# Output product of a state-space scan: seven block products per pair of tiles instead of eight

## The chip, the cores and the metric

The kernel runs on one core of a Trainium2 chip. The metric is the device time of one execution in microseconds. A core has a matrix engine (PE, with its weight loads listed as PEld), a vector engine (DVE), a scalar engine (ACT), a general engine (POOL) and a queue engine that here issues the loads (SP). Each engine runs its own instructions in the order in which they were placed on it, and waits on semaphores for the others.

## The reference, cut to what matters

The program is one layer: a graph part, a state-space scan, and a feed-forward part, each added to the residual `x`. The change lies in the scan alone. Of the scan this matters (16 sequences of 32 tokens, 512 model columns, 8192 inner columns in 8 groups of 1024):

```
proj = jnp.einsum('bsd,od->bso', h, in_proj_w)
gate = proj[..., :D_INNER]
hBC = jax.nn.silu(causal_conv(proj[..., D_INNER:D_INNER + CONV_DIM], conv_w, conv_b))
...
M = jnp.einsum('bcihn,bcjhn->bcijh', Ch, Bh) * jnp.transpose(L, (0, 2, 3, 4, 1))
Y_diag = jnp.einsum('bcijh,bcjhp->bcihp', M, hc)
...
y = (Y_diag + Y_off).reshape(b, S, H_M, P_M)[:, :s] + D_res
yg = y.reshape(b, s, D_INNER) * jax.nn.silu(gate)
ygr = yg.reshape(b, s, G_M, gsz)
ygr = ygr * jax.lax.rsqrt(jnp.mean(ygr * ygr, axis=-1, keepdims=True) + EPS)
y = ygr.reshape(b, s, D_INNER) * gnorm_w
out = jnp.einsum('bsd,od->bso', y, out_proj_w)
return residual + out
```

A sequence fits in one chunk, so no state passes between chunks. The last product, `out`, is 512 tokens by 8192 inner columns by 512 model columns in f32, and it is the one that the change computes in another way.

## The kernel before

**Tiling.** Inner columns lie on the 128 partitions and the 512 tokens along the free axis. The 8192 inner columns are 64 tiles of 128, and a group (`g`, of 8) is `TG` = 8 tiles. The 512 tokens are four quarters `q` of 128. `xt` holds the residual, tokens on partitions, one 512-column slice per quarter.

**A group's three steps.** `inner(g)` projects and convolves: for each of 8 tiles, `project` (L1114) loads a 256 KB weight tile `win` on SP (six buffers) and makes four f32 products into one of two PSUM buffers of tag `p`, once for the gate and once for the hidden part. The gate's product goes through a Silu on ACT (L1199) into `gs`; the hidden product through ACT (L1127), three shifted multiply-adds on DVE (L1132) and a Silu (L1135) into `hid`. `gs` and `hid` have two buffers each, so two groups are alive at a time.

`mix(g)` makes the scan's values: per tile `i`, four transposes of `hid` on PE (`pht`, L1228, PSUM tag `m`), a scaling on DVE (`hd`, L1230), every second tile a decay table (`decays`: `da` on POOL L1208, `pl` on PE L1213 in tag `m`, `ed` by an exponential on ACT L1218), two products `el` on DVE (L1241), sixteen half-width records on PE (`py`, L1249, PSUM tag `y`), then on DVE the skip term (L1253) and the gating (L1254), on ACT the square (L1256, L1259) and the scaling by the norm weight (L1261), and on POOL the sum of squares `ssq` (L1260).

`close(g)` makes the group's part of the output: the sum over partitions of `ssq` on PE (`pn`, L1268, tag `y`), the factor `rs` from it on DVE and ACT, eight loads of `out_proj` tiles on SP (`wo`, L1276, ten buffers), and for each quarter eight accumulating f32 products of 128 x 128 by 128 x 512 into a PSUM buffer of tag `o` (`po`, L1281), which DVE scales by `rs` and adds to `xt` (L1284).

**Order.** The text's order is `inner(0)`, and then for each `g`: `inner(g + 1)`, `mix(g)`, `close(g)`. The order on each engine is not written out by hand. A planner puts the instructions on their engines ahead of the run, and the text's order is its priority. The PSUM has eight banks and the four tags `p`, `m`, `y`, `o` take two each, so all are spoken for.

Of the kernel before, what the change touches and what calls it, by code (L numbers as in the profile page):

```python
# [8 lines left out]
F32 = mybir.dt.float32  # L9
# [4 lines left out]
ALU = mybir.AluOpType  # L14
# [4 lines left out]
P = 128  # L19
B = 16  # L20
C = 32
D = 512
# [18 lines left out]
H_M, G_M, SEQ = 128, 8, 32  # L41
D_INNER = 8192
NT = D_INNER // P
TG = NT // G_M
# [8 lines left out]
def kernel(ctx: ExitStack, tc: tile.TileContext, I, out):  # L53
# [68 lines left out]
    with ExitStack() as cx:  # L122
        scan_part(nc, tc, cx, I, id32, ones, xt, U, rstd, lows)
# [931 lines left out]
def scan_part(nc, tc, cx, I, id32, ones, xt, u, rstd, lows):  # L1055
# [3 lines left out]
    wk = cx.enter_context(tc.tile_pool(name="swk", bufs=2))  # L1059
    sm = cx.enter_context(tc.tile_pool(name="ssm", bufs=3))  # L1060
    wpool = cx.enter_context(tc.tile_pool(name="sw", bufs=4))
    ps_p = cx.enter_context(tc.tile_pool(name="sps_p", bufs=2, space=PSUM))
    ps_m = cx.enter_context(tc.tile_pool(name="sps_m", bufs=2, space=PSUM))
    ps_y = cx.enter_context(tc.tile_pool(name="sps_y", bufs=2, space=PSUM))
    ps_o = cx.enter_context(tc.tile_pool(name="sps_o", bufs=2, space=PSUM))
# [82 lines left out]
    with tc.tile_pool(name="soft", bufs=1) as sp:  # L1148
# [11 lines left out]
        s2 = sp.tile([P, 4, H_M], F32, name="s2")  # L1160
        nc.vector.tensor_tensor(s2, s, s, ALU.mult)
        acc = sp.tile([P, 4, H_M], F32, name="acc")
# [29 lines left out]
    def inner(g):  # L1192

        gs = big.tile([P, TG, D], F32, tag="gs", name=f"gs{g}")
        hid = big.tile([P, TG, D], F32, tag="hid", name=f"hid{g}")
        for i in range(TG):
            t = g * TG + i
            pg = project(t, f"g{t}")
            nc.scalar.activation(gs[:, i], pg, AF.Silu)  # L1199
            convolve(hid[:, i], t, f"h{t}")  # L1200
            if g > 0:
                next(parts, None)
        return gs, hid

    def decays(h):

        da = sm.tile([P, 4, 4, SEQ], F32, tag="da", name=f"da{h}", bufs=2)
        nc.gpsimd.tensor_tensor(  # L1208
            da, lei.unsqueeze(1).unsqueeze(1).to_broadcast([P, 4, 4, SEQ]),
            dA[:, :, h:h + 4].rearrange("p q h -> p h q").unsqueeze(3).to_broadcast([P, 4, 4, SEQ]), ALU.mult,  # L1210
        )
        pl = ps_m.tile([P, 4, 4, SEQ], F32, tag="m", name=f"pl{h}")
        nc.tensor.matmul(  # L1213
            pl.rearrange("p h q i -> p (h q i)"), lhsT=gt, rhs=da.rearrange("p h q i -> p (h q i)"),
            start=True, stop=True,
        )
        ed = sm.tile([P, 4, 4, SEQ], F32, tag="ed", name=f"ed{h}", bufs=2)
        nc.scalar.activation(ed, pl, AF.Exp)  # L1218
        return ed

    def mix(g, gs, hid):

        ssq = wk.tile([P, D], F32, tag="ssq", name=f"ssq{g}")
        for i in range(TG):
            t = g * TG + i
            pt = ps_m.tile([P, 4, P], F32, tag="m", name=f"pht{t}")
            for q in range(4):
                nc.tensor.transpose(pt[:, q], hid[:, i, q * P:(q + 1) * P], id32)  # L1228
            hd = sm.tile([P, 4, 2, 64], F32, tag="hd", name=f"hd{t}")
            nc.vector.tensor_tensor(  # L1230
                hd, pt.rearrange("p q (h c) -> p q h c", h=2),
                dt[:, :, 2 * t:2 * t + 2].unsqueeze(3).to_broadcast([P, 4, 2, 64]), ALU.mult,
            )
            py = ps_y.tile([P, 4, P], F32, tag="y", name=f"py{t}")
            if i % 2 == 0:
                decay = decays(2 * t)
            els = []
            for j in range(2):

                el = sm.tile([P, 4, P], F32, tag="el", name=f"el{2 * t + j}")  # L1240
                nc.vector.tensor_tensor(  # L1241
                    el.rearrange("p q (b i) -> p q b i", b=4),
                    decay[:, 2 * (i % 2) + j].unsqueeze(2).to_broadcast([P, 4, 4, SEQ]),
                    CB[:, g].rearrange("p q (b i) -> p q b i", b=4), ALU.mult,
                )
                els.append(el)
            for q in range(4):
                for j in range(2):
                    nc.tensor.matmul(  # L1249
                        py[64 * j:64 * j + 64, q], lhsT=hd[:, q, j], rhs=els[j][:, q], start=True, stop=True  # L1250
                    )
            pyf = py.rearrange("p q t -> p (q t)")
            nc.vector.scalar_tensor_tensor(hid[:, i], hid[:, i], dpc[:, t:t + 1], pyf, ALU.mult, ALU.add)  # L1253
            nc.vector.tensor_tensor(gs[:, i], gs[:, i], hid[:, i], ALU.mult)  # L1254
            if i == 0:
                nc.scalar.activation(ssq, gs[:, i], AF.Square)  # L1256
            else:
                sq = wk.tile([P, D], F32, tag="sq", name=f"sq{t}")
                nc.scalar.activation(sq, gs[:, i], AF.Square)  # L1259
                nc.gpsimd.tensor_tensor(ssq, ssq, sq, ALU.add)  # L1260
            nc.scalar.activation(gs[:, i], gs[:, i], AF.Copy, scale=gnw[:, t:t + 1])  # L1261
        return ssq

    def close(g, gs, ssq):

        pn = ps_y.tile([P, 4], F32, tag="y", name=f"pn{g}")
        for q in range(4):
            nc.tensor.matmul(pn[:, q:q + 1], lhsT=ssq[:, q * P:(q + 1) * P], rhs=ones[:, 0:1], start=True, stop=True)  # L1268
        mean = sm.tile([P, 4], F32, tag="gm", name=f"gm{g}")
        nc.vector.tensor_scalar(mean, pn, 1.0 / (TG * P), None, ALU.mult)  # L1270
        rs = sm.tile([P, 4], F32, tag="gr", name=f"gr{g}")
        rstd(sm, rs, mean, 4, f"gn{g}")
        wo = []
        for i in range(TG):
            w = wpool.tile([P, D], F32, tag="wo", name=f"wo{g}_{i}", bufs=TG + 2)
            nc.sync.dma_start(out=w, in_=I["out_proj"][g * TG + i])  # L1276
            wo.append(w)
        for q in range(4):
            po = ps_o.tile([P, D], F32, tag="o", name=f"po{g}_{q}")
            for i in range(TG):  # L1280
                nc.tensor.matmul(  # L1281
                    po, lhsT=gs[:, i, q * P:(q + 1) * P], rhs=wo[i], start=(i == 0), stop=(i == TG - 1)
                )
            nc.vector.scalar_tensor_tensor(xt[:, q], po, rs[:, q:q + 1], xt[:, q], ALU.mult, ALU.add)  # L1284

    cur = inner(0)
    for g in range(G_M):
        nxt = inner(g + 1) if g + 1 < G_M else None
        ssq = mix(g, *cur)
        close(g, cur[0], ssq)  # L1290
        cur = nxt


# [140 lines left out]
```

## Time and profile before

| | us |
|---|---|
| three executions | 2415.48, 2420.97, 2423.53 |
| median of them | 2420.97 |
| the profiled execution | 2416.21 |
| its span, first to last instruction | 2414.5 |
| mean granted clock of PE over the span | 0.971 of full speed |

The scan runs from about 1370 us of the span to 2316 us. The groups follow one another at an equal distance: the eight `pn` stand at

| group | 0 | 1 | 2 | 3 | 4 | 5 | 6 | 7 |
|---|---|---|---|---|---|---|---|---|
| `pn` at, us | 1612.71 | 1716.34 | 1821.40 | 1926.58 | 2031.63 | 2136.68 | 2241.81 | 2296.60 |

From group 1 to group 6 that is 105.1 us a group. The last distance is short because no group's projections are left. In a row of the groups of instructions, the first number after the bar is busy time, then the mean of one in ns, then the idle time of the engine ahead of them with the engine that ended it. In a row of the timeline the first two numbers are the start and the length, and records of one line that follow each other are merged (x8). Starts of the products overlap the ends of the ones before, so the price of one is the distance between starts.

### The profile page before, as it was taken

How to read it: one execution, taken by the hardware profiler on the slowest of the kernel's cores; microseconds unless marked ns; L12 is line 12 of the kernel's file. 1: busy time of each engine (PE TensorE's matmuls, PEld its weight loads, DVE VectorE, ACT ScalarE, POOL GpSimd, SP SyncE). 2: the span in 40 equal slices, each digit the busy share in tenths (PEclk: the TensorE clock that was granted, in tenths of full speed). 3: DMA queues.
4: the chain of work that ended last, by engine and by line, in shares of the span. 5: the costliest groups of instructions: out<-in, count | busy, mean ns of one | idle time of the engine just before them, and what ended most of it. 6: DMA issues, size and time to landing. Idle time of an engine off the chain costs nothing. (4 is left out here: it accounts for less than half of the span.)

```text
span 2414.5 us, 88867 instructions
## 1 busy us (share of the span) xinstructions
PE 2190.0 (91%) x39234; PEld 1248.1 (52%) x39234; DVE 1699.6 (70%) x3674; ACT 1100.1 (46%) x2023; POOL 831.6 (34%) x897
## 2 busy tenths in 40 slices
PE   5699798999999778789999789999999999999979
PEld 2255455667676454567777544444444444444422
DVE  8487797888899888889999866554553625446643
ACT  6677566667665334345555322333332424333331
POOL 2165556445446565664655300020210202021200
PEclk9799899999999999999999899999999999999989
DMA  1323232132132231422211212213112121210000
GB/s 48 80 55 77 48 80 57 43 73 47 36 70 56 54 77 46 91 52 65 63 34 41 91 53 77 75 32 91 53 53 71 35 91 46 73 55 20 27 36 18
DMA packets 121625, 137.99 MB, mean 57 GB/s; under 512 B 18398, under 2 KB 79506, under 8 KB 121154
## 3 DMA queue, kind: packets, MB, share of 16 engines
q1 hardware_dynamic: 121240, 132.32, 21.9%
q8 instruction: 308, 5.05, 0.9%
q14 instruction: 77, 0.63, 0.1%
HBM read 77.02 MB, written 12.85 MB: 37 GB/s over the span
## 5 line engine op out<-in xcount | busy, mean ns | idle before, releaser
L849 POOL TENSOR_TENSOR EN<-e,rz 128x480 f32<-128x480 f32 x344 | 342.4, 995 | 554.4 <-DVE rz L847 430.1
L874 PE MATMUL u<-WA,DD 128*32 128x128 bf16 (+1 forms) x16512 | 418.6, 250 | 26.4 <-issue 26.4
L874 PEld LDWEIGHTS <-DD 128*32 128x32 f16 x16512 | 338.8, 98 | 72.7 <-issue 68.5
L879 ACT COPY us<-u 128x512 f32<-128x512 f32 x516 | 302.0, 587 | 149.5 <-PE u L874 131.8
L834 ACT ACTIVATE e<-s,smc 128x480 f32<-128x480 f32 x344 | 227.6, 662 | 290.7 <-PE s L829 248.0
L770 POOL TENSOR_TENSOR DD<-fs,crep 128x480 f16<-128x480 f32 (+2 forms) x344 | 349.6, 1017 | 0.0
L902 PEld LDWEIGHTS h<-e,us 128*32 128x32 f32 (+1 forms) x11008 | 248.8, 126 | 144.1 <-issue 65.6
L902 PE MATMUL h<-e,us 128*32 128x30 f32 (+1 forms) x11008 | 282.0, 211 | 37.1 <-DVE e L855 19.4
L821 DVE TENSOR_REDUCE c<-s 128x16 bf16<-128x480 f32 x344 | 220.7, 642 | 107.0 <-PE s L812 104.4
L1132 DVE SCALAR_TENSOR_TENSOR cyh<-ppch,t_conv_w,cyh 128x496 f32<-128x496 f32 (+2 forms) x192 | 137.4, 716 | 221.7 <-ACT cyh L1127 217.7
L1208 POOL TENSOR_TENSOR da<-lei,dA 128x512 f32<-128x512 f32 x32 | 40.6, 1269 | 611.8 <-PE pl L1213 577.5
L1281 PE MATMUL po<-wo,gs 128*128 128x512 f32 x512 | 240.5, 605 | 10.4 <-DVE xt L1284 10.3
L1120 PE MATMUL ppch<-hT,winch 128*128 128x512 f32 x512 | 232.2, 593 | 0.0
L1120 PE MATMUL ppg<-hT,wing 128*128 128x512 f32 x512 | 231.9, 593 | 0.0
L855 DVE STREAM_TRANSPOSE e<-EN 128x512 f32<-128x512 f32 x344 | 224.4, 652 | 0.0
L841 DVE TENSOR_REDUCE z<-e 128x16 f32<-128x480 f32 x344 | 219.5, 638 | 0.0
L539 ACT ACTIVATE sgn<-kd 128x512 bf16<-128x512 f32 x256 | 153.0, 598 | 56.2 <-PE kd L538 52.4
L812 PEld LDWEIGHTS <-DD 128*32 128x32 f16 x5504 | 81.7, 96 | 163.2 <-issue 129.5
L723 DVE TENSOR_SCALAR oh<-it,rank 128x512 bf16<-128x512 f16 x512 | 158.0, 368 | 7.5 <-PE pp L689 7.5
L812 PE MATMUL s<-DX,DD 128*32 128x120 f16 x5504 | 143.1, 223 | 19.6 <-DMA DX<-DD 16.2
L1120 PEld LDWEIGHTS ppch<-hT,winch 128*128 128x128 f32 x512 | 93.7, 190 | 122.7 <-issue 122.3
L1120 PEld LDWEIGHTS ppg<-hT,wing 128*128 128x128 f32 x512 | 95.8, 190 | 114.0 <-issue 114.0
(327 smaller groups left out, 2845.6 us busy)
## 6 DMA issues: line engine op xcount, KB each, us to landing
DX<-DD SPq DMA_DIRECT2D x456, 90.0 KB
wo<-in_out_proj SPq DMA_DIRECT2D x64, 256.0 KB
wing<-in_in_proj SPq DMA_DIRECT2D x64, 256.0 KB
winch<-in_in_proj SPq DMA_DIRECT2D x64, 256.0 KB
crep<-dC SPq DMA_DIRECT2D x128, 64.0 KB
dS<-so SPq DMA_DIRECT2D x32, 256.0 KB
fs<-dS SPq DMA_DIRECT2D x128, 64.0 KB
wincB<-in_in_proj SPq DMA_DIRECT2D x8, 256.0 KB
```

The costliest lines, as they stand in the source:

```text
L770: nc.gpsimd.tensor_tensor(d[:, :, m0 - n0:n1 - n0], win, crep[:, :, m0:n1].unsqueeze(3).to_broadcast([P, 4, n1 - m0, K]), ALU.subtract,)
L812: nc.tensor.matmul(s[rh, j * 4 * QB:(j + 1) * 4 * QB].rearrange("p (b q) -> p b q", b=4), lhsT=d[:, h, c0:c0 + 32], rhs=dx[:, h, :, c0:c0 ...
L821: nc.vector.tensor_reduce(c, live["s", at, gi].rearrange("p (i q) -> p i q", q=QB), AX.X, ALU.max, negate=True)
L834: nc.scalar.activation(e, s.rearrange("p (i q) -> p i q", q=QB), AF.Exp, scale=smc)
L841: nc.vector.tensor_reduce(z, e, AX.X, ALU.add)
L849: nc.gpsimd.tensor_tensor(en[:, :, :QB], e, rz.unsqueeze(2).to_broadcast([P, NI, QB]), ALU.mult)
L855: nc.vector.transpose(e.rearrange("p i q -> p (i q)"), en.rearrange("p i q -> p (i q)"))
L874: nc.tensor.matmul(u[rh, jj], lhsT=d[:, h, c0:c0 + 32], rhs=WA[k][:, h].rearrange("p b o -> p (b o)"), start=(jj == 0 and k == 0), stop=(k ...
L879: nc.scalar.copy(us[:, j - jj:j + 1], u)
L902: nc.tensor.matmul(h[r:r + co, pr, q0:q0 + QB], lhsT=us[:, j, b * co:(b + 1) * co], rhs=e[:, 4 * j + b, :QB], start=npair > 1, stop=True, ...
L1120: nc.tensor.matmul(pp, lhsT=w[:, k], rhs=hT[:, k], start=(k == 0), stop=(k == 3))
L1281: nc.tensor.matmul(po, lhsT=gs[:, i, q * P:(q + 1) * P], rhs=wo[i], start=(i == 0), stop=(i == TG - 1))
```

## The change

In place of eight block products for each pair of tiles and each half of the tokens, the change makes seven and gets the four output blocks from sums of them (the scheme with 15 sums). For a pair of tiles `i0`, `i1`, and the quarters 2h and 2h + 1, the blocks of the left operand are `a11`, `a21` (tile `i0`, the two quarters) and `a12`, `a22` (tile `i1`), and those of the right operand are the 256-column halves of the two `wo` tiles. `operands` makes four sums on DVE for the left side (`s1`, `s2`, `s4` and in place `a21`), for both values of h at once, and four for the right side (`t1`, `t2`, `t4` and in place `b12`), each of 256 elements a partition. It is called for pairs 0, 1 and 2 inside `mix`, at tiles 2, 4 and 6, and for pair 3 in `close`.

The seven products are accumulated over the four pairs, in seven halves of four PSUM banks for each h: both banks of tags `p` and `m` for h = 0, of `o` and `y` for h = 1. At the end one ACT copy and eleven DVE instructions for each h combine them and add them, scaled by `rs`, to `xt`. The `wo` loads move from `close` ahead of `mix`, with eight buffers for ten. `da` and `ed` have one buffer for two, and `hd` two for three.

```diff
-        da = sm.tile([P, 4, 4, SEQ], F32, tag="da", name=f"da{h}", bufs=2)
+        da = sm.tile([P, 4, 4, SEQ], F32, tag="da", name=f"da{h}", bufs=1)
...
-        ed = sm.tile([P, 4, 4, SEQ], F32, tag="ed", name=f"ed{h}", bufs=2)
+        ed = sm.tile([P, 4, 4, SEQ], F32, tag="ed", name=f"ed{h}", bufs=1)
...
-            hd = sm.tile([P, 4, 2, 64], F32, tag="hd", name=f"hd{t}")
+            hd = sm.tile([P, 4, 2, 64], F32, tag="hd", name=f"hd{t}", bufs=2)
...
+            if i and i % 2 == 0:
+                pairs.append(operands(g, i // 2 - 1, gs, wo))
...
-        for q in range(4):
-            po = ps_o.tile([P, D], F32, tag="o", name=f"po{g}_{q}")
-            for i in range(TG):
-                nc.tensor.matmul(
-                    po, lhsT=gs[:, i, q * P:(q + 1) * P], rhs=wo[i], start=(i == 0), stop=(i == TG - 1)
-                )
-            nc.vector.scalar_tensor_tensor(xt[:, q], po, rs[:, q:q + 1], xt[:, q], ALU.mult, ALU.add)
+    def tokens(gs, i, r):
+        return gs[:, i].rearrange("p (a r t) -> p r a t", a=2, r=2)[:, r]
+    def weights_of(g):
+        wo = []
+        for i in range(TG):
+            w = wpool.tile([P, D], F32, tag="wo", name=f"wo{g}_{i}", bufs=TG)
+            nc.sync.dma_start(out=w, in_=I["out_proj"][g * TG + i])
+            wo.append(w)
+        return wo
+    def operands(g, p, gs, wo):
+        i0, i1 = 2 * p, 2 * p + 1
+        a11, a21, a12, a22 = (tokens(gs, i, r) for i in (i0, i1) for r in (0, 1))
+        S = sm.tile([P, 3, 2, P], F32, tag="osum", name=f"osum{g}_{p}", bufs=TG // 2)
+        s1, s2, s4 = (S[:, k] for k in range(3))
+        nc.vector.tensor_tensor(s1, a21, a22, ALU.add)
+        nc.vector.tensor_tensor(s2, s1, a11, ALU.subtract)
+        nc.vector.tensor_tensor(a21, a11, a21, ALU.subtract)
+        nc.vector.tensor_tensor(s4, a12, s2, ALU.subtract)
+        b11, b12, b21, b22 = (w[:, k * HN:(k + 1) * HN] for w in (wo[i0], wo[i1]) for k in (0, 1))
+        T = sm.tile([P, 3, HN], F32, tag="wsum", name=f"wsum{g}_{p}", bufs=TG // 2)
+        t1, t2, t4 = (T[:, k] for k in range(3))
+        nc.vector.tensor_tensor(t1, b12, b11, ALU.subtract)
+        nc.vector.tensor_tensor(t2, b22, t1, ALU.subtract)
+        nc.vector.tensor_tensor(b12, b22, b12, ALU.subtract)
+        nc.vector.tensor_tensor(t4, b21, t2, ALU.subtract)
+        return [(a11, b11), (a12, b21), (s4, b22), (a22, t4), (s1, t1), (s2, t2), (a21, b12)]
+    def close(g, gs, ssq, wo, pairs):
+        pairs.append(operands(g, TG // 2 - 1, gs, wo))
+        acc = []
+        for h in range(2):
+            banks = [
+                pool.tile([P, 2, HN], F32, tag=tag, name=f"po{g}_{h}_{tag}{k}")
+                for pool, tag in (((ps_p, "p"), (ps_m, "m")), ((ps_o, "o"), (ps_y, "y")))[h] for k in range(2)
+            ]
+            acc.append([banks[k // 2][:, k % 2] for k in range(7)])
+            for p, products in enumerate(pairs):
+                for k, (x, y) in enumerate(products):
+                    nc.tensor.matmul(
+                        acc[h][k], lhsT=x[:, h], rhs=y, start=(p == 0 and k % 2 == 0), stop=(p == TG // 2 - 1),
+                        skip_group_check=True,
+                    )
+            if h == 0:
...
+        for h in range(2):
+            p1, p2, p3, p4, p5, p6, p7 = acc[h]
+            t0, t1 = (wk.tile([P, D], F32, tag="sq", name=f"ou{g}_{h}_{k}") for k in range(2))
+            u2, u3, c = t0[:, :HN], t0[:, HN:], t1[:, :HN]
+            def add_to(q, half, v):
+                x = xt[:, 2 * h + q, half * HN:(half + 1) * HN]
+                nc.vector.scalar_tensor_tensor(x, v, rs[:, 2 * h + q:2 * h + q + 1], x, ALU.mult, ALU.add)
+            nc.scalar.copy(c, p1)
+            nc.vector.tensor_tensor(u2, c, p6, ALU.add)
+            nc.vector.tensor_tensor(c, c, p2, ALU.add)
+            add_to(0, 0, c)
+            nc.vector.tensor_tensor(u3, u2, p7, ALU.add)
+            nc.vector.tensor_tensor(u2, u2, p5, ALU.add)
+            nc.vector.tensor_tensor(u2, u2, p3, ALU.add)
+            add_to(0, 1, u2)
+            nc.vector.tensor_tensor(c, u3, p4, ALU.add)
+            add_to(1, 0, c)
+            nc.vector.tensor_tensor(u3, u3, p5, ALU.add)
+            add_to(1, 1, u3)
     cur = inner(0)
     for g in range(G_M):
         nxt = inner(g + 1) if g + 1 < G_M else None
-        ssq = mix(g, *cur)
-        close(g, cur[0], ssq)
+        wo = weights_of(g)
+        ssq, pairs = mix(g, *cur, wo)
+        close(g, cur[0], ssq, wo, pairs)
         cur = nxt
```

What stands at "if h == 0" is the old text of `pn` and `rs`, unchanged, now between the products of the two halves.

## The prediction

> **What bounds the kernel now.** I read the page's first parts, then the groups of instructions, then one whole group of the scan in order of time, engine by engine, and last the busy time by stretch. The change touches the scan alone, so the graph part ahead of it and the feed-forward part behind keep their time. The groups give the price of what is replaced.
>
> ```profile
> L1281 PE MATMUL po<-wo,gs 128*128 128x512 f32 x512 | 240.5, 605 | 10.4 <-DVE xt L1284 10.3
> L1120 PE MATMUL ppch<-hT,winch 128*128 128x512 f32 x512 | 232.2, 593 | 0.0
> ```
>
> The program has 256 output products (8 groups, 4 quarters, 8 tiles) and the profile 512 records: an f32 product is two records. Their durations overlap, so the price is the distance between starts: eight L1120 records take 3.60 us and the last 0.593, so (3.60 - 0.593) / 7 = 0.43 us for 512 columns. One group's output is 64 x 0.43 = 27.5 us of PE.
>
> The windows cut the group from 1735 us into three stretches (columns: us; busy time of PE, PEld, DVE, ACT, POOL; clock; DMA).
>
> ```profile
> 1735.10:1785.20 50.10, 50.10 (x120) 21.91 (x119) 15.80 (x22) 13.96 (x22) 0.00 (x0) 1.00 0.31 91
> 1785.20:1819.20 34.00, 34.00 (x200) 17.62 (x199) 31.45 (x43) 17.11 (x23) 13.60 (x10) 1.00 0.06 16
> 1819.20:1840.10 20.90, 19.66 (x51) 8.72 (x51) 3.16 (x10) 5.61 (x7) 1.27 (x1) 1.00 0.22 64
> ```
>
> First 50 us of projections for the next group: PE is solid and DVE busy 16 of 50. Then 34 us of mixing: DVE is busy 31.5, nearly without a hole. PE looks full, yet it holds filler there. Then a tail of 21 us in which DVE does almost nothing and PE finishes the output. The granted clock is full in all three. So the span of a group is a PE stretch, a DVE stretch and a PE stretch, and work is dear or free by the stretch in which it lands. What PE does in the mixing:
>
> ```profile
> 1786.76 1.88 PE L1120 MATMUL ppg<-hT,wing 128*128 128x512 f32 x4
> ...
> 1790.23 1.12 PE L1120 MATMUL ppg<-hT,wing 128*128 128x512 f32 x2
> ...
> 1792.84 1.02 PE L1120 MATMUL ppg<-hT,wing 128*128 128x512 f32 x2
> ...
> 1795.31 1.88 PE L1120 MATMUL ppch<-hT,winch 128*128 128x512 f32 x4
> ```
>
> These 12 records are projections of the group after next (the 8 of one gate tile, half of a hidden tile; the other half starts at 1840.14). Their text stands behind `close`, so the planner puts on an engine whatever has its inputs and a free buffer, earlier text first. They are 12 x 0.43 = 5.2 us that the next projection stretch need not do: 50 in place of 16 x 8 x 0.43 = 55. The tail:
>
> ```profile
> 1821.40 1.05 PE L1268 MATMUL pn<-ones,ssq 128*128 128x1 f32 x8
> 1822.31 2.82 PE L1281 MATMUL po<-wo,gs 128*128 128x512 f32 x6
> 1826.31 14.00 PE L1281 MATMUL po<-wo,gs 128*128 128x512 f32 x32 [1.18 <-DVE xt L1284]
> 1840.14 1.88 PE L1120 MATMUL ppch<-hT,winch 128*128 128x512 f32 x4
> ```
>
> Quarters 2 and 3 wait for a bank of `ps_o` and then run alone for 14 us.
>
> **Seven products on PE.** 56 products of 256 columns, 112 records, replace 64 of 512. No f32 row has 256 columns; the nearest is L1185 with 128:
>
> ```profile
> 1429.53 1.05 PE L1185 MATMUL pcb<-Cg,Bg 128*128 128x128 f32 x8
> ```
>
> Eight in 1.05 us with a last one of 0.275 is 0.111 apart. From 0.111 at 128 and 0.43 at 512 the line gives 0.215 to 0.217 at 256: 112 x 0.215 = 24.1 us, 3.4 less per group. Bounds: 0.215 and 0.30 (0.111 and a whole 0.19 us weight load unhidden), which is 33.6. I take 0.215, since at 128 columns loads of 0.19 us already sit under products 0.111 apart.
>
> The rule that speaks against this: the Trainium skill, TensorE: Matmul & The Clock Gate, Part 3, The mechanism, says that a weight load overlaps a running product only when the two use different row groups. By it the 48 added loads would cost 48 x 0.19 = 9 us a group; the trace disagrees, with full-height products 0.111 apart under 0.19 us loads.
>
> PE's total is not what ends a group, so 3.4 is not the gain. The stretches are.
>
> **DVE in the mixing.** Each pair of tiles adds four operand sums of 256 columns (S) and four of weights (T). A 512-column sum lasts 0.68 and starts 0.60 after its forerunner; L919 has 0.325 at 160 columns and 0.642 at 480, so 256 last about 0.41 and start 0.33 apart, longer where one needs the last. I take 0.37. Three pairs' S sums land in the mixing, where nothing covers them: 12 x 0.37 = 4.4 us a group, 35.5 in eight. Bounds: 2.3 (12 x 0.33 less the 1.7 us that DVE waits before the last L1253) and 7.1 (12 x 0.59, each held 0.18 by POOL as L1241 is, 0.857 on average against 0.68).
>
> The formula for an f32 sum in VectorE: DVE Perf Modes of the Trainium skill, section The TRN2 errata, gives an estimate of 0.424 us at 256, and 12 of them 5.1; at 512 it says 0.69 where this trace has 0.68.
>
> **T sums** need only `wo`, which loads from the end of the last tail. I cost them at nothing: 16 x 0.37 = 5.9 us under 34 us of idle DVE in the projections. Without that cover they cost 5.9 a group, 47 in all. The cover has an edge: a hidden tile's bank is released 0.78 (ACT) + 2.2 (three L1132) + 0.2 after its products, and PE returns to it after 3.43, so a conv late by over 0.25 us stops PE.
>
> **The moved loads and smaller pools.** `wo` has eight buffers in place of ten, so all eight issues (0.33 us each, about 6 in a row on SP) wait for the last products of the group before. Behind them on SP stand the `win` loads; six buffers cover 6 x 3.43 = 20.6 us. A T sum that waits for `wo` has convolutions queued behind it on DVE, and ACT and PE wait for those. One `ed`: the next exponential (0.60 and two hand-overs, about 0.9) waits for the pair's last L1241; an L1254 and an L1230 (1.28) stand between. One `da` and two `hd` I cost at nothing by the same cover. For all of it: between 0 and 3.6 us a group (four uncovered exponentials, or a late load); I take 0.5, near the lower end, as both covers exceed what they cover: 4 us.
>
> **The tail.** From the last L1254's end to the next projection it is 20.9 us. Square and scale take 1.5 (1819.2 to 1820.7). Now nearly half of the products run inside the mixing: pairs 0 to 2 in `ps_p` and `ps_o` (24 products), then `ps_m`. PE's own mixing work is some 1.8 us of a 4.2 us tile, so about 30 of 56 fit and 26 remain: 26 x 0.43 = 11.2, with pn 0.9 and gaps 0.2: 13.8. Gain 7.1 in each of seven tails: 49.7. Bounds: 23 remain (12.5) or all 56 (26.7). The first half's adds (11 of 0.37, a copy) lie under the second half's products, the second half's under the next projections. In the last group nothing covers these: 13.8 + 0.6 + 4.1 = 18.5 against 2294.4 to 2316.3, 21.9: gain 3.4.
>
> **The filler.** The first half's sums take both buffers of tag `p`, ahead of the next-but-one projections. If those could still go first, their gate activation would need a `gs` buffer, held until this group's products are done (L1199 waited 14.4 us for L1281), and these would need the two banks: a circle. So buffers must be granted in text order, and the 12 records leave the mixing: 5.2 us in six groups, 31. Bounds 0 and 31; by the circle, 31.
>
> **Sum.** 35.5 + 4 + 31 - 49.7 - 3.4 = +17.4 us. The profiled execution took 2416.2 (span 2414.5, 1.7 around it): 2433.6. The median shown is 4.8 above it, and on it this is 2438.
>
> **Rivals.**
> Filler kept: 17.4 - 31 = -13.6, 2407, faster. It decides as soon as less than 2.3 us a group of the 5.2 is lost. For it: the planner's filling in the rows above; against: the circle. 0.16.
> PE's sum sets the end, the stretches overlapping: 8 x -3.4 = -27, 2394. Against: PE is solid in the projections, so mixing cannot slip in. 0.09.
> T sums stay in the mixing: +47, 2485. For: they are written there; against: the early filler shows that text place does not hold. 0.12.
> DVE stands at late `wo` or `ed`: 3 us a group in place of 0.5, +20, 2458. For: 0.25 us of slack; against: 14 us of tail for the loads. 0.13.
> The products don't enter the mixing: tails of 26.7, 8 x 12.9 = +103, 2541. 0.04.
>
> **How the numbers follow.** The forecast has 0.46 and its own range is 2424 to 2456 (S sums and tail between their nearer bounds). The range 2404 to 2482 leaves out the second rival, the last and half of the third, near 0.18. A difference under 0.3% (7 us) can't be told from no change. Faster: the first two rivals less what ends near 2414, 0.23. Same: the forecast's low edge and that rest, 0.13. Slower 0.64.
>
> **What would show it.** Right: product records 0.215 apart; a mixing of 38 to 39 us with L1254's end as its end; a tail of 13 to 14; projection stretches of 55 with no L1120 inside the mixing; T sums among the L1132. Wrong: L1120 still in the mixing; T sums there; PE idle for DVE in the projections; a period under 105.1.

## The result, and the profile after

| | before | after |
|---|---|---|
| median of six runs, us | 2420.39 | 2450.81 |
| lowest to highest, us | 2412.85 to 2423.53 | 2436.94 to 2454.88 |
| ratio, with its 95% interval | | 1.0122 [1.0092, 1.0152] |
| profiled execution, us | 2416.21 | 2453.84 |
| its span, us | 2414.5 | 2452.1 |

The changed kernel is 1.2% slower. The forecast was 2438, slower, within 2404 to 2482. The two spans differ by 37.6 us. Of these 4.0 lie ahead of the scan, in a part that the change does not touch: the start of the scan (its first record of the `pd` products) scatters between 1377 and 1392 us over the runs of this study, whatever the kernel. The rest lies in the scan and follows from the groups' distance, which has grown from 105.1 to 109.2 us: the eight `pn` of the changed kernel stand at 1626.23, 1736.31, 1845.51, 1954.71, 2063.91, 2173.11, 2282.30 and 2340.57. The six distances from group 0 to group 6 bring 27.0 us, the stretch up to group 0's `pn` 9.5 (2.6 of it only because `pn` now stands later in the tail), the last distance 3.5, and the last tail gives 7.3 back; 0.9 lie behind the scan.

The price of a product first. Three of the groups of instructions of the changed kernel (busy time, mean in ns, idle time before):

```profile
L1315 PE MATMUL po_p<-wo,gs 128*128 128x256 f32 x128 | 41.6, 408 | 0.0
L1315 PE MATMUL po_o<-wo,gs 128*128 128x256 f32 x128 | 36.4, 386 | 0.0
L1315 PE MATMUL po_m<-wsum,osum 128*128 128x256 f32 x128 | 35.3, 396 | 1.9 <-DVE osum L1289 1.9
```

L1315 is the product's line in the changed kernel, and its ten groups have 896 records, 112 for each group of the scan. One is 0.379 us long.

The end of group 2 in PE's order of time (start, length, records merged):

```profile
1842.29 0.69 PE L1315 MATMUL po_p<-wo,gs 128*128 128x256 f32 x2
1843.22 1.16 PE L1315 MATMUL po_m<-wsum,osum 128*128 128x256 f32 x4 [0.24 <-DVE osum L1289]
...
1845.51 0.95 PE L1322 MATMUL pn<-ones,ssq 128*128 128x1 f32 x8
1846.32 1.11 PE L1315 MATMUL po_y<-wsum,osum 128*128 128x256 f32 x4
1847.26 0.59 PE L1315 MATMUL po_y<-wo,gs 128*128 128x256 f32 x2
1847.69 1.03 PE L1315 MATMUL po_y<-wsum,osum 128*128 128x256 f32 x4
1848.56 0.59 PE L1315 MATMUL po_y<-wo,gs 128*128 128x256 f32 x2
```

Four records from 1847.69 and two from 1848.56: 0.87 us for four starts, so 0.217 apart, and two in 0.43 from 1847.26 to 1847.69. That is the 0.215 of the forecast; a group's products take 24.1 us of PE where they took 27.5. The weight loads, one of 0.19 us for each record, are all hidden under it. The Trainium skill, TensorE: Matmul & The Clock Gate, Part 3, The mechanism, says in its list of what overlaps that a load overlaps a running product only where the row groups differ; ahead of the list it also lets a load go first that fills the background weight buffer. These are full-height products with full-height loads, and their starts stay 0.217 us apart, so the measurement decides against the list's rule.

The same three stretches of group 2 as before: projections, mixing, tail (us; busy PE, PEld, DVE, ACT, POOL; clock; DMA):

```profile
1744.54:1799.47 54.93, 54.93 (x129) 23.83 (x128) 21.83 (x41) 14.29 (x23) 0.00 (x0) 1.00 0.28 80
1799.47:1840.74 41.27, 33.98 (x228) 23.05 (x227) 37.99 (x55) 16.97 (x23) 12.84 (x10) 1.00 0.04 14
1840.74:1853.74 13.00, 12.76 (x63) 10.73 (x63) 9.44 (x30) 5.91 (x9) 1.27 (x1) 1.00 0.37 104
```

Against 50.10, 34.00 and 20.90: the projections have grown by 4.8, the mixing by 7.3, the tail has shrunk by 7.9. The clock is granted in full in all three, as before. The projections hold all 128 records of L1120, a whole group's worth, and the mixing has none that starts in it; 12 had started there before. So the filler is gone. The mixing is a DVE stretch still (38 of 41 us busy), only longer, and PE waits in it. Of the group's 112 product records 53 start in the tail and 59 in the mixing; the forecast had 52 and 60.

### The profile page after: what moved, and what is told of

It reads as the page before. It is cut to its first block, busy times and chain, and to the rows that moved or that the text cites. A ratio compares the mean times of both kernels' runs of the same rounds, so it can differ in the third digit from the quotient of the medians.

```text
span 2452.1 us, 90128 instructions
## 1 busy us (share of the span) xinstructions
PE 2181.4 (89%) x39618; PEld 1324.7 (54%) x39618; DVE 1846.0 (75%) x4074; ACT 1103.2 (45%) x2039; POOL 822.9 (34%) x897
## 5 line engine op out<-in xcount | busy, mean ns | idle before, releaser
L821 DVE TENSOR_REDUCE c<-s 128x16 bf16<-128x480 f32 x344 | 220.7, 641 | 106.5 <-PE s L812 103.9
L1120 PE MATMUL ppch<-hT,winch 128*128 128x512 f32 x512 | 230.7, 593 | 0.0
L1120 PE MATMUL ppg<-hT,wing 128*128 128x512 f32 x512 | 230.2, 592 | 0.0
L539 ACT ACTIVATE sgn<-kd 128x512 bf16<-128x512 f32 x256 | 153.0, 598 | 58.3 <-PE kd L538 54.4
L1120 PEld LDWEIGHTS ppg<-hT,wing 128*128 128x128 f32 x512 | 97.3, 190 | 119.9 <-issue 119.5
L1120 PEld LDWEIGHTS ppch<-hT,winch 128*128 128x128 f32 x512 | 93.6, 190 | 125.0 <-issue 123.5
L829 PE MATMUL s<-c,idb 128*128 128x480 bf16 x344 | 131.5, 382 | 7.1 <-issue 3.6
```

What stands on the lines that cost most here:

```text
L821: nc.vector.tensor_reduce(c, live["s", at, gi].rearrange("p (i q) -> p i q", q=QB), AX.X, ALU.max, negate=True)
L1120: nc.tensor.matmul(pp, lhsT=w[:, k], rhs=hT[:, k], start=(k == 0), stop=(k == 3))
```

## The experiments

Three lengths are used for every run, all from group 2 or a middle group where they repeat to 0.1 us: the mixing, from the first `hd` on DVE (L1230 before) to the end of the last gating (L1254); the tail, from there to the end of the last output record (0.2 us past the windows' tail, whose bound is the next start); and the period, from `pn` to `pn`. The ratio is to the kernel before, run on the same chip with it.

| kernel | mixing | tail | period | ratio |
|---|---|---|---|---|
| before | 33.7 | 21.1 | 105.1 | 1 |
| after | 40.6 | 13.15 | 109.2 | 1.0122 [1.0092, 1.0152] |
| e1, before with the small pools | 35.3 | 21.1 | 106.7 | 1.0040 [1.0022, 1.0059] |
| e2, after without left sums | 35.4 | 15.65 | 106.5 | 1.0082 [1.0066, 1.0097] |
| e3, after without right sums | 40.6 | 13.15 | 109.2 | 1.0116 [1.0093, 1.0140] |
| e4, before without filler | 33.4 | 21.45 | 110.2 | 1.0148 [1.0133, 1.0163] |
| e5, eight products, first half in tag `p` | 33.4 to 34.3 | 20.0 | 109.3 | 1.0093 [1.0071, 1.0115] |
| e6, after without POOL's sum | 38.1 | 14.2 | 107.7 | one execution, 2435.51 us |
| e7, before without POOL's sum | 34.9 | 18.1 | 103.5 | one execution, 2402.49 us |
| e8, before with the stages side by side | | 25.7 | 100.1 | 0.9843 [0.9825, 0.9861] |
| e9, after with the stages side by side | | 22.3 | 96.7 | 0.9785 [0.9762, 0.9807] |

The mixing and the projections are one stretch in e8 and e9, of 67.07 us in both.

**e4: the filler alone.** In the kernel before, `pn` is made in two parts in the two buffers of tag `p`, so that these are asked for in `close`, ahead of the next-but-one projections. Nothing else changes.

```diff
-        pn = ps_y.tile([P, 4], F32, tag="y", name=f"pn{g}")
-        for q in range(4):
-            nc.tensor.matmul(pn[:, q:q + 1], lhsT=ssq[:, q * P:(q + 1) * P], rhs=ones[:, 0:1], start=True, stop=True)
...
-        nc.vector.tensor_scalar(mean, pn, 1.0 / (TG * P), None, ALU.mult)
+        for c in (0, 2):
+            pn = ps_p.tile([P, 2], F32, tag="p", name=f"pn{g}_{c}")
+            for q in range(2):
+                nc.tensor.matmul(
+                    pn[:, q:q + 1], lhsT=ssq[:, (c + q) * P:(c + q + 1) * P], rhs=ones[:, 0:1], start=True, stop=True
+                )
+            nc.vector.tensor_scalar(mean[:, c:c + 2], pn, 1.0 / (TG * P), None, ALU.mult)
```

> The kernel before, with pn computed in two parts in the two buffers of tag p, so that later projections cannot go first; all else as before. My step: no L1120 in the mixing, projections of 55 us, 5.2 us more in each of six groups: 31 us more, 2451. Rival: PE makes up for it elsewhere and the time stays within 7 us of before.

2447.24 against 2411.72 us, 35.5 more. The distance of `pn` is 110.2 in most groups, 5.1 more than before (two are longer still, 111.2 and 112.6). All the records of L1120 between 1786 and 1848 us in PE's timeline of this kernel, with `pn`:

```profile
1785.50 2.74 PE L1120 MATMUL ppch<-hT,winch 128*128 128x512 f32 x6
1824.62 1.05 PE L1270 MATMUL pn<-ones,ssq 128*128 128x1 f32 x8 [0.40 <-POOL ssq L1260]
1843.37 3.60 PE L1120 MATMUL ppg<-hT,wing 128*128 128x512 f32 x8
1846.80 1.45 PE L1120 MATMUL ppch<-hT,winch 128*128 128x512 f32 x3
```

The six at 1785.50 are the last of the group's own projections. After them no projection starts until the output is done at 1843.37. So here the buffers of a tag went out in the order of the text: what asks for them in `close` shuts out the later users until then, and the holes of the DVE-bound stretch aren't filled with PE's next work. This costs 5.1 us a group without any of the seven products.

**e3: the right sums.** The four sums of `wo` halves are left out.

```diff
-        T = sm.tile([P, 3, HN], F32, tag="wsum", name=f"wsum{g}_{p}", bufs=TG // 2)
-        t1, t2, t4 = (T[:, k] for k in range(3))
-        nc.vector.tensor_tensor(t1, b12, b11, ALU.subtract)
-        nc.vector.tensor_tensor(t2, b22, t1, ALU.subtract)
-        nc.vector.tensor_tensor(b12, b22, b12, ALU.subtract)
-        nc.vector.tensor_tensor(t4, b21, t2, ALU.subtract)
+        t1, t2, t4 = b12, b22, b21
```

> The changed kernel with the four right sums of each pair left out (products read the unsummed weights). My step: they lie under idle DVE time, so nothing changes: 2446 to 2453, the mixing 40.6 us, the projections 55. Rival: they cost 3 us or more a group by late weights or late convolutions, 2425 or less.

The time itself is 2438.29 us where 2446 to 2453 were expected, but the kernel before, run beside it, stood at 2411.72 where it had been 2420.39; the ratio is that of the changed kernel within its interval. Mixing, tail and period stay to 0.05 us what they are in the changed kernel, so the right sums are free in the middle groups. The last distance of `pn`, with no projections to hide anything, is shorter (53.8 for 58.3): there they cost 4.5 us, once. Where they went in a middle group, on DVE in the changed kernel, early in the next projections:

```profile
1750.24 0.42 DVE L1297 TENSOR_TENSOR wsum<-wo,wsum 128x256 f32<-128x256 f32 x1
1750.58 0.42 DVE L1298 TENSOR_TENSOR wo<-wo,wo 128x256 f32<-128x256 f32 x1
1750.92 0.42 DVE L1299 TENSOR_TENSOR wsum<-wo,wsum 128x256 f32<-128x256 f32 x1
1752.42 2.22 DVE L1132 SCALAR_TENSOR_TENSOR cyh<-ppch,t_conv_w,cyh 128x496 f32<-128x496 f32 x3 [1.08 <-ACT cyh L1127]
```

They start 0.34 apart, and the convolution behind them still finds DVE idle for 1.08 us, waiting for ACT and not for a sum. Ahead of group 7 it is the first `hd` that comes behind them, and one of them waits for a late `wo`:

```profile
2291.48 0.42 DVE L1297 TENSOR_TENSOR wsum<-wo,wsum 128x256 f32<-128x256 f32 x1 [0.52 <-DMA wo<-in_out_proj]
...
2292.15 1.29 DVE L1298 TENSOR_TENSOR wo<-wo,wo 128x256 f32<-128x256 f32 x1
...
2294.75 0.68 DVE L1231 TENSOR_TENSOR hd<-pht,dt 128x512 f32<-128x512 f32 x1
```

This `hd` starts 4.05 us after the last output product of group 6; without the right sums (e3) it is 1.51, and in the kernel before 0.71.

**e1: the small pools.** The kernel before, with one buffer for `da` and for `ed` and two for `hd`. (The way round, the changed kernel with the old sizes, wasn't tried.)

```diff
-        da = sm.tile([P, 4, 4, SEQ], F32, tag="da", name=f"da{h}", bufs=2)
+        da = sm.tile([P, 4, 4, SEQ], F32, tag="da", name=f"da{h}", bufs=1)
...
-        ed = sm.tile([P, 4, 4, SEQ], F32, tag="ed", name=f"ed{h}", bufs=2)
+        ed = sm.tile([P, 4, 4, SEQ], F32, tag="ed", name=f"ed{h}", bufs=1)
...
-            hd = sm.tile([P, 4, 2, 64], F32, tag="hd", name=f"hd{t}")
+            hd = sm.tile([P, 4, 2, 64], F32, tag="hd", name=f"hd{t}", bufs=2)
```

> The kernel before, with one da, one ed and two hd buffers and nothing else of the change. My step: the exponential is covered by the two DVE operations between, so 0 to 4 us more, 2420 to 2425, and a mixing of 33.7 us as before. Rival: the single ed leaves four uncovered exponentials of 0.9 us in each mixing: mixing 37 us, 29 us more in all, 2449.

The mixing is 1.6 us longer, and so is the period: neither the expected 33.7 nor the rival's 37. The time is 7.3 us longer, where 0 to 4 were expected. It is not an uncovered exponential. DVE's groups in one mixing of the kernel before, and then of e1 (the last number but one is the mean in ns):

```profile
L1241 DVE TENSOR_TENSOR el<-ed,CB 128x512 f32<-128x512 f32 x16 | 13.2, 838 | 0.0
L1254 DVE TENSOR_TENSOR gs<-gs,hid 128x512 f32<-128x512 f32 x8 | 7.2, 900 | 0.0
L1253 DVE SCALAR_TENSOR_TENSOR hid<-hid,t_Dp,py 128x512 f32<-128x512 f32 x8 | 5.9, 741 | 2.1 <-PE py L1249 2.0
```

```profile
L1241 DVE TENSOR_TENSOR el<-ed,CB 128x512 f32<-128x512 f32 x16 | 14.1, 900 | 0.8 <-PE py L1249 0.8
L1254 DVE TENSOR_TENSOR gs<-gs,hid 128x512 f32<-128x512 f32 x8 | 8.5, 1067 | 0.1
L1253 DVE SCALAR_TENSOR_TENSOR hid<-hid,t_Dp,py 128x512 f32<-128x512 f32 x8 | 5.9, 740 | 0.7 <-PE py L1249 0.7
```

No DVE instruction waits for `ed` here, and DVE's idle time shrinks (2.1 to 0.8 + 0.7). ACT does stand for the single buffer, until DVE's last `el` has read it; in the kernel before, its exponentials waited for PE's `pl` alone:

```profile
1788.65 0.60 ACT L1218 ACTIVATE ed<-pl 128x512 f32<-128x512 f32 x1 [0.62 <-DVE el L1241]
...
1804.47 0.60 ACT L1218 ACTIVATE ed<-pl 128x512 f32<-128x512 f32 x1 [1.90 <-DVE el L1241]
```

What grows on DVE are the two operations whose inputs both lie in SBUF: 0.9 us more in the products, 1.3 in the gatings. L1253, which reads `py` from PSUM, keeps its 0.74. Both are operations that POOL's work can hold (see e2). That the smaller pools shift them onto it is my reading of these rows; it wasn't tried by itself.

**e2: the left sums.** The four sums of the `gs` blocks are left out.

```diff
-        S = sm.tile([P, 3, 2, P], F32, tag="osum", name=f"osum{g}_{p}", bufs=TG // 2)
-        s1, s2, s4 = (S[:, k] for k in range(3))
-        nc.vector.tensor_tensor(s1, a21, a22, ALU.add)
-        nc.vector.tensor_tensor(s2, s1, a11, ALU.subtract)
-        nc.vector.tensor_tensor(a21, a11, a21, ALU.subtract)
-        nc.vector.tensor_tensor(s4, a12, s2, ALU.subtract)
+        s1, s2, s4 = a21, a22, a12
```

> The changed kernel with the four left sums of each pair left out (products read the unsummed blocks). My theory: the left sums are the whole of the longer mixing, so it falls from 40.6 us to about 33.7 and the tail from 13.2 to about 12: 8 x 8.2 = 66 us less than the changed kernel, 2385. Rival: part of the longer mixing is the small pools or products in front of the scan's own on PE; then the mixing stays at 37 or more and the time above 2410.

The theory that the left sums are the whole of the loss has fallen: without them the kernel is still 0.8% slower than before. The mixing is 5.2 us shorter than in the changed kernel, which is their price there; the 1.7 that still stands above 33.7 agrees with the small pools' 1.6 (e1), so the rival named a true part but made it too large. And 2.5 of the 5.2 come back in the tail, because fewer products fit into a shorter mixing (15.65 for 13.15). So taking the sums away is worth 2.7 us a group, not 5.2.

How twelve sums of 0.41 us with starts 0.33 apart come to 5.2 is seen at pair 1. DVE in the changed kernel, and then POOL at the same time:

```profile
1823.21 0.82 DVE L1289 TENSOR_TENSOR osum<-gs 128x256 f32<-128x256 f32 x1
1823.95 0.68 DVE L1257 TENSOR_TENSOR gs<-gs,hid 128x512 f32<-128x512 f32 x1
1824.55 1.29 DVE L1290 TENSOR_TENSOR osum<-osum,gs 128x256 f32<-128x256 f32 x1
1825.77 1.48 DVE L1291 TENSOR_TENSOR gs<-gs 128x256 f32<-128x256 f32 x1
1827.17 0.41 DVE L1292 TENSOR_TENSOR osum<-gs,osum 128x256 f32<-128x256 f32 x1
```

```profile
1822.28 1.46 POOL L1263 TENSOR_TENSOR ssq<-ssq,sq 128x512 f32<-128x512 f32 x1 [3.28 <-ACT sq L1262]
1824.08 1.48 POOL L1208 TENSOR_TENSOR da<-lei,dA 128x512 f32<-128x512 f32 x1 [0.33 <-PE pl L1213]
1825.52 1.44 POOL L1263 TENSOR_TENSOR ssq<-ssq,sq 128x512 f32<-128x512 f32 x1
```

L1289, L1290 and L1291 are held until the POOL instruction that began before each is through (`ssq`, `da` and `ssq`, ending at 1823.74, 1825.56 and 1826.96), and end 0.28 to 0.29 us after it. L1292 has POOL idle beside it and takes 0.41. The Trainium skill, SBUF — State Buffer, Who interferes with whom, says that a DVE instruction with two SBUF inputs and a GpSimd instruction that reads SBUF take a shared port in turns, the later one waiting for the whole of the other. These rows agree, and so does L1253 above, which has one SBUF input and was never held. PE pays at the same spot, as its next records show:

```profile
1824.83 0.59 PE L1315 MATMUL po_o<-wo,gs 128*128 128x256 f32 x2
1827.63 0.70 PE L1315 MATMUL po_p<-wo,osum 128*128 128x256 f32 x2 [2.21 <-DVE osum L1292]
```

PE stands for 2.21 us for a pair's last sum, in the middle of the stretch that was to be filled with its products.

**e6 and e7: POOL's sum of squares left out**, in the changed kernel and in the one before, to split the price of the left sums into their own length and the hold.

```diff
-                nc.gpsimd.tensor_tensor(ssq, ssq, sq, ALU.add)
```

> The kernel before without POOL's additions to the sum of squares. L1241 and L1254, 0.84 and 0.90 us on average in the mixing, fall towards 0.68, and the mixing from 33.7 us by about 4 to 29 or 30. Rival: what holds them is not POOL; they and the mixing stay.

> The changed kernel without POOL's additions to the sum of squares (only the first tile's square counts). To be read against the same cut in the kernel before. My theory: a part of the price of the left sums is that DVE is held while POOL works; without it the mixing is 5.6 us longer than that of the cut kernel before (1.6 for the pools, 4.0 for twelve sums 0.33 apart). Rival: POOL has no part, and the difference stays 6.9.

In the kernel before, the mean of the 16 `el` falls from 838 to 736 ns:

```profile
L1241 DVE TENSOR_TENSOR el<-ed,CB 128x512 f32<-128x512 f32 x16 | 11.6, 736 | 0.0
```

The rest of the expectation was missed. The gatings stay at 0.90 us (two of the eight take 1.56 beside POOL's `da`), and the mixing doesn't fall to 29 or 30. Up to the seventh gating it takes 29.8 us where it took 30.5, but the last gating comes late, and with it the mixing is 34.9 us where it was 33.7. Its end on DVE:

```profile
1810.38 0.68 DVE L1254 TENSOR_TENSOR gs<-gs,hid 128x512 f32<-128x512 f32 x1
1812.37 0.16 DVE L1269 TENSOR_SCALAR gm<-pn 128x4 f32<-128x4 f32 x1 [1.31 <-PE pn L1267]
...
1814.36 0.75 DVE L1253 SCALAR_TENSOR_TENSOR hid<-hid,t_Dp,py 128x512 f32<-128x512 f32 x1 [1.62 <-PE py L1249]
...
1815.48 0.69 DVE L1254 TENSOR_TENSOR gs<-gs,hid 128x512 f32<-128x512 f32 x1
```

Without the adds `pn` waits for no sum, and it is placed ahead of the last tile's end. So leaving the adds out changes the order as well as the hold; the tail is 3.0 us shorter in return and the period 1.6. In the changed kernel the order moves too: the mixing is 38.1 us, with DVE waiting 2.20 us for `py` ahead of the last tile's skip term, and the period is 1.5 shorter. The two mixings are then 3.2 us apart, under both the 5.6 and the 6.9 of the expectation, but the two tails have come nearer by as much (3.9 for 7.9), and the periods are 4.2 apart where they were 4.1. That POOL has a part shows in the records: the twelve left sums last 7.9 us in all in the changed kernel and 6.7 in e6. How the 5.2 us divide, the two runs don't tell.

**e5: eight products with the banks of the change.** If more banks are what lets products enter the mixing, the kernel before might do the same with its eight: quarters 0 and 1 go to tag `p`, 2 and 3 to tag `o`.

```diff
-            po = ps_o.tile([P, D], F32, tag="o", name=f"po{g}_{q}")
+            pool, tag = ((ps_p, "p"), (ps_o, "o"))[q // 2]
+            po = pool.tile([P, D], F32, tag=tag, name=f"po{g}_{q}")
```

> The kernel before with eight products, but the four quarters in four banks (two of tag p, two of o), so that all may enter the mixing and the filler cannot. My theory: the shorter tail of the changed kernel comes from products that enter the mixing as well as from their smaller number. PE has room for 11 to 14 us of them, so of 27.5 us some 15 remain and the tail is 17 to 18 us; mixing 33.7, projections 55: 106 to 107 us a group against 105.1, 7 to 14 us more in all. Rival: the banks alone do it and the tail falls to 13: 102 us a group, 15 to 20 us faster than before. Other rival: nothing enters that did not before, the tail stays 21: 110 us, 30 us slower.

The tail shrinks by 1.1 us only, not by the 3 to 4 expected, and the period is 109.3, not 106 to 107. That nearly equals the changed kernel's 109.2. So with the filler lost in both, the seven products and all that they bring are a wash: 6.9 us gained in the tail (20.0 to 13.15), 6.9 paid in the mixing (33.7 to 40.6). The whole difference to the kernel before is then the lost filler, less the 1.1 us that the added banks alone give.

**e8 and e9: the stages side by side.** If the period is long because a PE-bound and a DVE-bound stretch stand one after the other, the eighth product was taken from an engine that had time in hand anyway. So `inner(g + 1)` is split: its tiles are projected one by one from within `mix(g)`, at the start of each tile. e8 does it to the kernel before, e9, with the same lines, to the changed one.

```diff
-        for i in range(TG):
+
+        def tile_of(i):
...
-        return gs, hid
+
+        return (gs, hid), tile_of
...
-    def mix(g, gs, hid):
+    def mix(g, gs, hid, ahead):
...
+            if ahead:
+                ahead(i)
...
-    cur = inner(0)
+    cur, tile_of = inner(0)
+    for i in range(TG):
+        tile_of(i)
...
-        nxt = inner(g + 1) if g + 1 < G_M else None
-        ssq = mix(g, *cur)
+        nxt, ahead = inner(g + 1) if g + 1 < G_M else (None, None)
+        ssq = mix(g, *cur, ahead)
```

> The kernel before, with the text of the next group's projections moved tile by tile into the mixing. My theory: what sets a group is the sequence of a PE stretch and a DVE stretch; PE needs about 98 us a group (55 projections, 27.5 output, 15 scan) and DVE 52, so side by side a group takes 98 to 100 us in place of 105.1: 7 x 5 to 7, 35 to 50 us less, 2361 to 2376 on this chip's 2411. Rival: the planner already fills PE, and the table switches of ACT between Silu and Exp take the gain: within 10 us of before or slower.

> The changed kernel with the same move. My theory: side by side PE's sum counts, and seven products need 3.4 us a group less than eight, while DVE has room for the sums (about 70 us of 95): 95 to 98 us a group, 10 to 25 us under the eight products interleaved. Rival: the tail with all eight banks taken, 20 us and more when no product has been made early, adds idle PE, or late sums hold PE: 100 us or more a group, no faster than the eight products interleaved.

2377.81 and 2360.92 us against 2416.51, as expected. One period of e8 and then of e9, by stretch: projections beside mixing, tail, and the next two projected tiles ahead of the next `hd`.

```profile
1725.83:1792.90 67.07, 67.07 (x283) 32.84 (x282) 42.03 (x64) 36.06 (x49) 11.95 (x10) 1.00 0.20 59
1792.90:1818.57 25.67, 25.67 (x67) 11.81 (x66) 3.24 (x10) 5.71 (x8) 1.27 (x1) 1.00 0.19 57
1818.57:1825.91 7.34, 7.34 (x21) 3.45 (x21) 0.75 (x2) 1.03 (x2) 0.00 (x0) 1.00 0.42 125
```

```profile
1718.69:1785.76 67.07, 67.07 (x290) 34.09 (x289) 46.67 (x76) 36.02 (x49) 11.93 (x10) 1.00 0.20 59
1785.76:1808.06 22.30, 22.30 (x109) 19.74 (x108) 10.59 (x32) 6.45 (x10) 1.27 (x1) 1.00 0.26 73
1808.06:1815.41 7.35, 7.35 (x22) 3.46 (x21) 6.24 (x19) 1.03 (x2) 0.00 (x0) 1.00 0.32 102
```

PE is now busy in every microsecond of all six rows, so the period is PE's own work: 100.1 us with eight products, 96.7 with seven. The difference is 3.4 us, the 27.5 less 24.1 that the seven products save. In e9's first stretch DVE has 20 us to spare, and the twelve left sums cost nothing there: it is as long as in e8. The last group, with no projections beside it, still shows what the change puts on DVE: its mixing is 41.06 us in e9 and 32.99 in e8. That is not the left sums alone, since right sums and the adds of the group before lie in it as well; in the changed kernel the same mixing is 41.07, without the right sums (e3) 39.13 and without the left ones (e2) 35.52.

```profile
L1246 DVE TENSOR_TENSOR el<-ed,CB 128x512 f32<-128x512 f32 x16 | 10.3, 684 | 2.8 <-PE py L1254 2.8
L1294 DVE TENSOR_TENSOR osum<-osum,gs 128x256 f32<-128x256 f32 x3 | 1.3, 424 | 0.1
```

These are DVE's groups in e9's first stretch: `el` takes 684 ns for the 914 in the changed kernel's mixing, and this sum 424 for 911. So in the longer stretch DVE's operations are hardly held any more. e9 is the fastest of all the kernels run here.

## Why the prediction was right, point by point

The forecast, slower, came true, and its mechanism is what the runs show. The sign hung on one term, the lost filler: without its 31 us the same sum gives faster, and e4 shows that term by itself. Of the medians' 30 us the forecast had 17: three terms were too small, and a tail that came out better than forecast made up for a part of them. A group's account from the experiments, each with its run:

| term, us a group | forecast | measured | from |
|---|---|---|---|
| lost filler | +5.2 | +5.1 | e4 |
| left sums in the mixing | +4.4 | +5.2 | e2 |
| small pools and moved loads | +0.5 | +1.6 | e1 |
| right sums in the middle groups | 0 | 0.0 | e3 |
| tail | −7.1 | −7.9 | windows |
| sum | +3.0 | +4.0 | the period shows 109.2 − 105.1 = +4.1 |

- **The products' price** of 0.215 was right, from two row lengths that lay on both sides of it.
- **The lost filler** was right in cause and size. The circle argued from `gs` and the banks was not tested; what e4 shows is the plainer half of it, that a buffer asked for earlier in the text is not lent out first.
- **The right sums** were rightly costed at nothing in the middle groups, with the convolutions still waiting for ACT behind them; the edge of 0.25 us that the text named was not reached there. For the last group the step was wrong: it has no projections to cover them, and they cost 4.5 us there (e3), near the 5.9 that the text had for uncovered ones.
- **The tail** was forecast at 13.8 us by products that no longer fit: 52 records left, and 53 were. It measures 13.0, since the 1.5 us of square and scale, which the forecast left empty on PE, are filled with products of earlier pairs (PE is busy 12.76 of the 13.00).
- **The left sums** were mis-sized. The forecast took 0.37 us each, between 0.33 unheld and 0.59 with POOL's hold, and 5.2 / 12 = 0.43 was measured. The hold on a short operation isn't the share that a long one shows: a 256-column sum that meets a POOL instruction waits for all of it, 0.41 becoming up to 1.48.
- **The small pools** were mis-sized too: 1.6 and not 0.5, within the bounds of 0 to 3.6. The step that failed is that only an uncovered exponential or a late load was counted as their price. The cover held for DVE (no `el` of a middle group waits for `ed`), and yet DVE's `el` and gatings got longer by 2.2 us, by my reading through a changed meeting of DVE and POOL. The moved loads cost nothing visible in the middle groups: the last seven of a group's eight `wo` issues take 13.5 us from 1840.76, and no convolution waits behind them.
- **The last tail**: 17.2 us from the last gating's end to the end of the scan, forecast 18.5.

The two terms that are too small in every group make 8 × (0.8 + 1.1) = 15 us more, the seven tails 7 × 0.8 = 6 less, and the last tail 1 less: the forecast's 17.4 becomes 26, where the scan shows 32.7 (37.6 less 4.0 ahead of it and 0.9 behind). What is left lies at the two ends of the scan, which the forecast priced like the middle. At the last group it is the right sums' 4.5. The lost filler is not the cause there: in e4 and e5, which lose it too, group 7's first `hd` comes 0.71 us after the output of group 6, as in the kernel before. From group 0 to group 1 it is 2.4, whose cause was not looked for.

Of the rivals, the kept filler is refuted by the windows, the T sums in the mixing (of the middle groups) by e3, the products that don't enter by the tail of 13, and a DVE that stands at late `wo` or `ed` by its idle time: in the whole changed kernel the `el` waited 1.4 us for `ed`, one right sum 0.5 for `wo`, and no convolution for either. "PE's sum sets the end" is false for this change and true for another order: in e8 and e9 it is exactly what sets the period. What stays open is how the left sums' 5.2 us divide into their own length and the time held by POOL: the runs that were to tell (e6 and e7) changed the order as well.

## What to carry to other kernels

Price a saved instruction by the stretch that it is taken from: seven products for eight saved 3.4 us of PE a group; that brought nothing while PE had to wait for DVE, and all of it once the DVE-bound stage stood beside the PE-bound one in the text. Ask of every new user of a PSUM tag which later work used that tag to fill holes: here that cost more than the change could bring. And put two stages with different bounds side by side before making either cheaper.

## What the runs showed of the hardware that was not expected

Beside POOL's elementwise work, DVE's operations with two SBUF inputs that begin second were held until the POOL instruction was through, whatever their own length: 0.41 us became 0.82, 1.29 and 1.48 at pair 1. Taking such an operation away does not free the time that it was held: without the left sums (e2), the mean of the `el` in the mixing rises from 914 to 1044 ns and that of the gatings from 681 to 798; by my reading POOL's instructions then meet those instead. Of POOL's seven adds a group six fall into the mixing of the kernel before, and with them its 16 `el` take 1.6 us more in all than without (13.2 for 11.6, e7). And smaller buffer pools cost 1.6 us a group (e1) though in the mixing DVE never stood for `ed`, whose buffer had become single: ACT did.
